# Turning the causal attention result to token-major by VectorE squares and a store and load through memory, in place of TensorE transposes

## The chip, the cores and the metric

The kernel runs on one core of one Trainium2 chip, in fp32. The metric is the device time of one execution in microseconds; the number to compare is the median of several executions. A core has TensorE (PE, with its weight loads listed as PEld), VectorE (DVE), ScalarE (ACT), GpSimd (POOL) and SyncE (SP), which here issues nearly all DMAs. Each engine works through its own queue in order.

## The reference, cut to what matters

A batch is 128 channels by 48 x 48 positions, that is 2304 tokens of 128 channels. There are 8 batches. For each of them:

```python
# layer 0
x1 = x + causal_attention(group_norm(x))      # q, k, v: leaky_relu of projections with position rows
# layer 1, over tokens t = x1 as [2304, 128]
t1 = t + softmax(n @ n.T) @ n                 # n = layer_norm(t)
t2 = t1 + ffn(layer_norm(t1))                 # projection, batch norm over all tokens, sigmoid recurrence over tokens
```

In the causal attention, `out[n] = sum over m <= n of softmax(q_n . k_m / sqrt(128)) v_m`. What matters for the change is its last step: the result comes out with channels on the partitions, but it is added to `x`, and normalized over the channels, with tokens on the partitions.

## The kernel before, in words

A batch is cut into 6 chunks of 384 tokens (`NQ`, `QC`), a chunk into 3 blocks of 128 (`QB`). A batch has a causal part (class `Causal`, layer 0) and a full part (class `Full`, the attention of layer 1). Both work on items: a pair of one query chunk `j` and one key block `m`. An item is a score product `s` (line 980), an exponential on ScalarE into a tile `p` (982), for blocks on the diagonal a mask on POOL (985), and a product with the values into the PSUM tile `o` (991). The scores lie transposed, keys on the partitions, so `o` has channels on the partitions and tokens along the free dimension. The sum of the exponentials, which softmax divides by, is gathered on VectorE: every `p` is added to `acc` (1002, 1006). Chunk `j` of the causal part has 3(j+1) items. The tiles `p` come from a pool of 6, the PSUM tiles of scores and projections from one of 4 (`psum_s`), small results and transposes from one of 2 (`psum_t`), `o` from one of 2. A fp32 matmul is two passes of TensorE in the trace.

When a causal chunk is complete, `after` copies `o` to SBUF on ScalarE (1015, in the order that makes later 32 x 32 blocks fit), starts the load of the token-major `x` of that chunk (`x_tok`, 1019), and adds a chain of six steps:

- `turn`: VectorE turns `acc` in squares of 32 and sums the rows (1023, 1025);
- `sums`: a small TensorE matmul `dn` sums over the squares, VectorE takes the reciprocal `ri` (1031 to 1036);
- `residual`: TensorE transposes the three blocks of the copy into PSUM (`oc_t`, 931), VectorE multiplies by `ri` and adds `x` (1042), and takes mean and variance (912, 913);
- `rooted`: POOL takes the root (921);
- `normed`: VectorE normalizes into `xhT` (926);
- `back`: TensorE transposes to channel-major (`tb`, 931), ScalarE copies it (1061).

The full part needs the normalized chunks of the same batch. It has a chain of its own for each finished chunk, with the same transposes (`of_t`), and spreads and fetches tiles by DMA through memory (1248 to 1257).

The order of the queues is written out by hand: the program emits instructions in the order in which a small planner, `Stream`, runs the steps. `stream` lists the items of all batches, and the product of an item comes three items after its scores (`LAG`). The planner keeps a clock `now`, advanced by the columns of each matmul (`US` each), and for VectorE, ScalarE and POOL a time from which they are free (`free`). A chain's step has a cost in TensorE time and a list of engine times; it may run when its time `at` has come, at most two steps per item, the oldest chain first. So changed steps or costs shift the order of the other instructions too. `chunk_tile` hands out a tile from a tag's ring and first runs the chain of the tile's earlier holder up to a given step, so that a tile is not taken before its readers are in the queues.

The causal part of a batch starts while the full part of the batch before is still ending: the projections of the new batch (`project`, 871 to 886), its first chunks, and the last chain of the old batch meet there.

VectorE's `transpose` turns each 32 x 32 square by itself. A 128 x 128 block so turned still has its 16 squares in the old places.

Of the kernel before, what the change touches and what calls it, by code (L numbers as in the profile page):

```python
# [14 lines left out]
F32 = mybir.dt.float32  # L15
AF = mybir.ActivationFunctionType
ALU = mybir.AluOpType
# [587 lines left out]
def fast_path(ctx: ExitStack, tc: tile.TileContext, x, pe, w_ffn, out, x_tok, w_qkv, w_pos, v_t, gamma_beta, flag):  # L605
    nc = tc.nc
    B, C, H, W = x.shape
    N = H * W
    P = 128
# [52 lines left out]
    with ExitStack() as actx:  # L662
# [107 lines left out]
        for r in roots:  # L770
            nc.gpsimd.memset(r, 0.0)

        st = Stream()
        order = ExitStack()
        order.enter_context(tc.manual_schedule())
# [5 lines left out]
        def group_norm(b):  # L781
            xt = xbuf[b]
            c = {}

            def part1():
                gs = small2.tile([P, NQ, 6], F32, tag="gn_st", name=f"gn_st_{b}")
                for j in range(NQ):
                    nc.vector.bn_stats(gs[:, j, :], xt[:, ts(j, QC)])
                mv = small.tile([P, 2], F32, tag="gn_mv", name=f"gn_mv_{b}")
                nc.vector.bn_aggr(mv, gs)  # L790
                c["mv"] = mv

            def part2():
                mv = c["mv"]
                tp = psum_t(f"gn_m_{b}")
                nc.tensor.matmul(tp[:, 0:1], grp, mv[:, 0:1], start=True, stop=True)
                mg = small.tile([P, 1], F32, tag="gn_mg", name=f"gn_mg_{b}")
# [3 lines left out]
                e = small.tile([P, 1], F32, tag="gn_e", name=f"gn_e_{b}")  # L801
                nc.vector.scalar_tensor_tensor(e, d, d, mv[:, 1:2], ALU.mult, ALU.add)
                c["mg"], c["e"] = mg, e

            def part3():
                tp = psum_t(f"gn_v_{b}")
                nc.tensor.matmul(tp[:, 0:1], grp, c["e"], start=True, stop=True)
                rs = small.tile([P, 1], F32, tag="gn_rs", name=f"gn_rs_{b}")
                rsqrt(small, rs, tp[:, 0:1], 1e-5, "gn")
# [90 lines left out]

        def bounds(b):

            qk = small.tile([P, 2], F32, tag="qk", name=f"qk_{b}")
# [47 lines left out]
        class Causal:  # L951
# [37 lines left out]
            def product(self, j, m, o, p, ready, first, last):  # L989
                b, off = self.b, self.offset(j, m)  # L990
                nc.tensor.matmul(o[:, off:QC], vals[b][:, ts(m, P)], p[:, off:], start=first, stop=last)  # L991
                st.spend((QC - off) * US, ready)

                if first:
                    self.sums[j] = (p, None)
                    return
                if self.sums[j][1] is None:
                    self.whose[j] = {}
                    a = chunk_tile("acc", f"acc_{b}_{j}", self.whose[j], 1)
                    if off:  # L1000
                        nc.vector.tensor_copy(a[:, :off], self.sums[j][0][:, :off])
                    nc.vector.tensor_add(a[:, off:], self.sums[j][0][:, off:], p[:, off:])
                    self.sums[j] = (None, a)
                else:
                    a = self.sums[j][1]
                    nc.vector.tensor_add(a[:, off:], a[:, off:], p[:, off:])  # L1006
                st.then(ready, [("DVE", 0.15 + (QC - off) * 0.00105)])

            def after(self, j, o):
# [1 line left out]
                cols = ts(j, QC)  # L1011
                acc = self.sums.pop(j)[1]
                c = self.whose.pop(j)
                o_sb = chunk_tile("o", f"oc_{b}_{j}", c, 3)
                nc.scalar.copy(by_block(o_sb), o[:, :QC].rearrange("p (a g r) -> p a g r", a=R, g=QB))
                at = st.then(st.now, [("ACT", 0.5)])

                y = t1p.tile([P, QC], F32, tag="t1t", name=f"t1t_{b}_{j}")
                nc.sync.dma_start(y, x_tok[b, j])
# [17 lines left out]
                    c["ri"] = ri  # L1037

                def residual():
                    to = transposed(o_sb, f"oc_t_{b}_{j}")  # L1040
                    for g in range(QB):
                        nc.vector.scalar_tensor_tensor(
                            y[:, ts(g, P)], to[:, ts(g, P)], c["ri"][:, g : g + 1], y[:, ts(g, P)], ALU.mult, ALU.add
                        )
                    t1_tok[b, j] = y
                    c["mv"], c["ve"] = moments(y, f"c{b}_{j}", "l1")
# [25 lines left out]
        class Full:  # L1072
# [115 lines left out]
            def after(self, j, o):  # L1188
                b, rows, tsum = self.b, self.rows, self.tsum
                cols = ts(j, QC)  # L1190
                c = {}
                o_sb = chunk_tile("o", f"of_{b}_{j}", c, 2)
                nc.scalar.copy(o_sb, o[:, :QC])
                at = st.then(st.now, [("ACT", 0.5)])
                last = b == B - 1 and j >= NQ - 2

                def sums():

                    dn = small.tile([P, QB], F32, tag="dn", name=f"dn_{b}_{j}")
                    nc.vector.tensor_reduce(dn, rows[:, QB * j : QB * (j + 1), : j + 1], AX.X, ALU.add)  # L1200
                    n = NQ - 1 - j
                    if n:
                        tp = psum_t(f"ts_{b}_{j}")
                        k = n * R * QB
                        nc.tensor.matmul(
                            tp[:, :k], same.rearrange("p a c -> p (a c)"), tsum[j][:, :n, :].rearrange("p n k -> p (n k)"),
                            start=True, stop=True,
                        )
                        own = small2.tile([P, NQ - 1, R, QB], F32, tag="own", name=f"own_{b}_{j}")
                        nc.vector.tensor_mul(  # L1210
                            own[:, :n].rearrange("p n a g -> p (n a g)"), tp[:, :k], mine[:, :n].rearrange("p n a g -> p (n a g)")
                        )
                        more = small.tile([P, QB], F32, tag="more", name=f"more_{b}_{j}")
                        nc.vector.tensor_reduce(more, own[:, :n].rearrange("p n a g -> p g (n a)"), AX.X, ALU.add)
                        nc.vector.tensor_add(dn, dn, more)
                    ri = small.tile([P, QB], F32, tag="ri", name=f"ri_{b}_{j}")
                    nc.vector.reciprocal(ri, dn)
                    c["ri"] = ri

                def residual():  # L1220
                    tp = transposed(o_sb, f"of_t_{b}_{j}")
                    t2 = chunk_tile("t2", f"t2_{b}_{j}", c, 5 if last else 2, bufs=1)
                    for g in range(QB):
                        nc.vector.scalar_tensor_tensor(  # L1224
                            t2[:, ts(g, P)], tp[:, ts(g, P)], c["ri"][:, g : g + 1], t1_tok[b, j][:, ts(g, P)], ALU.mult, ALU.add
                        )
                    c["t2"] = t2
                    c["mv"], c["ve"] = moments(t2, f"f{b}_{j}", "l2")
                    if not last:
                        c["tt"] = chunk_tile("turn", f"tt_{b}_{j}", c, 5, bufs=1)  # L1230
# [20 lines left out]
                        nc.sync.dma_start(d[r], c["tt"][ts(r, SQ)].rearrange("c (k f) -> c k f", k=R))  # L1251

                def fetch():
                    c["t2x"] = chunk_tile("t2x", f"t2x_{b}_{j}", c, 7, bufs=1)
                    nc.sync.dma_start(c["t2x"], t2_d[:, b, cols])
                    c["scale"] = chunk_tile("scale", f"scale_{b}_{j}", c, 8, bufs=1)
                    nc.sync.dma_start(c["scale"], c["rs_d"][0].partition_broadcast(P))

                def product():
# [56 lines left out]
                else:  # L1316
# [5 lines left out]
                        (stored, 0.0, [("ACT", 0.85)]),  # L1322
                    ]
                c["chain"] = self.before["chain"] = st.add([
                    (sums, 0.15, [("DVE", 0.8)]),
                    (residual, 0.35, [("DVE", 3.2)]),
                    (rooted, 0.0, [("POOL", 0.9)]),
                    *steps,
                ], max(at, st.free["DVE"]) + 0.2 - st.now)
# [236 lines left out]
```

## Time and profile before

| | |
|---|---|
| median of 3 executions | 1795.67 us (1794.95 to 1795.85) |
| profiled execution, its own time | 1795.9 us |
| its span | 1793.8 us |
| mean granted TensorE clock | 0.991 |
| PE busy | 1757.0 us, 98% |
| DVE busy | 1298.0 us, 72% |
| ACT busy | 751.6 us, 42% |
| POOL busy | 217.0 us, 12% |
| DMA moved | 240.35 MB, 134 GB/s over the span |

The span runs from the first to the last instruction of the profiled execution; its own time is 2.1 us more. A row of a group of instructions names the line, the engine, the operation, the tiles `out<-in`, the shape and the count, then the busy time, the mean duration of one in ns, and the idle time of the engine ahead of them with what ended it. A matmul's duration is longer than the distance to the next one, since matmuls are pipelined; distances are read from the starts in a timeline. A row of a wait says who waited for whom, the sum in us, the number of times and the longest.

### The profile page before, as it was taken

Reading aid. Unit: us, or ns where it says so; the run is one execution under the profiler, and the core shown is the slowest. Engines: PE = TensorE matmul, PEld = TensorE weight load, DVE = VectorE, ACT = ScalarE, POOL = GpSimd, SP = SyncE. Lnnn points to the kernel's source line nnn. Section 1 sums busy time; section 2 is a strip of 40 time slices with the busy share of each in tenths; the row PEclk is TensorE's granted clock in tenths of the full one; section 3 lists DMA queues with packets and bytes.
Section 4 is the critical chain, followed back from the end, with each engine's and each line's share of the span. In section 5 each row is a group of like instructions: output and inputs, shape, how many; then the busy total and the mean of one; then the engine's idle time right before and its main releaser. Section 6 shows DMA issues by size and latency. Waiting matters only on the chain.

```text
span 1793.8 us, 22009 instructions
## 1 busy us (share of the span) xinstructions
PE 1757.0 (98%) x6363; PEld 1106.4 (62%) x6363; DVE 1298.0 (72%) x3321; ACT 751.6 (42%) x1852; POOL 217.0 (12%) x305
## 2 busy tenths in 40 slices
PE   8999999999999999999999999999999999999995
PEld 5666566665666566665666656665666656665574
DVE  5768668766887668686687668876686866876477
ACT  2344434443345424444344433454234443444354
POOL 1100011000210002000110002100020001100016
PEclk8999999999999999999999999999999999999998
DMA  4205662257314583056622573145830566025857
GB/s 151 102 1 190 180 166 82 74 181 192 109 62 132 162 217 106 1 188 179 167 83 74 182 187 113 63 132 163 216 106 1 183 183 172 27 72 182 201 179 200
DMA packets 176774, 240.35 MB, mean 134 GB/s; under 512 B 66209, under 2 KB 146242, under 8 KB 176644
## 3 DMA queue, kind: packets, MB, share of 16 engines
q1 hardware_dynamic: 175692, 235.83, 44.7%
q0 software_dynamic: 720, 2.62, 1.0%
q8 instruction: 53, 0.87, 0.2%
q14 instruction: 77, 0.63, 0.1%
q10 hardware_dynamic: 232, 0.40, 0.1%
HBM read 142.37 MB, written 96.41 MB: 133 GB/s over the span
## 4 chain that ended last, share of the span: by engine, by line
PE 95%; DVE 2%; DMA 1%; SPq 1%; issue 1%; ACT 0%; POOL 0%; DVEq 0%; ACTq 0%; POOLq 0%
PE s L1168 18%; PE o L1182 18%; PE s L980 17%; PE o L991 16%; PE o L1178 12%; PE pj L871 4%; PE pj L874 2%; PE z L1483 2%; PE wx L1264 2%; PE oc_t L931 1%; PE tb L931 1%; PE of_t L931 1%; SPq L1102 1%; DVE r L1465 0%; PE pb L829 0%
## 5 line engine op out<-in xcount | busy, mean ns | idle before, releaser
L1170 ACT ACTIVATE p<-s,shift 128x384 f32<-128x384 f32 x504 | 293.1, 582 | 491.3 <-PE s L1168 482.4
L982 ACT ACTIVATE p<-s 128x384 f32<-128x384 f32 (+2 forms) x504 | 233.0, 463 | 426.2 <-PE s L980 389.1
L1168 PE MATMUL s<-xh 128*128 128x384 f32 x1008 | 410.3, 489 | 0.0
L1182 PE MATMUL o<-p,xhT 128*128 128x384 f32 x1008 | 403.9, 487 | 4.4 <-ACT p L1170 4.4
L980 PE MATMUL s<-q,k 128*128 128x384 f32 (+2 forms) x1008 | 381.4, 460 | 0.1
L991 PE MATMUL o<-p,vT 128*128 128x384 f32 (+2 forms) x1008 | 378.3, 457 | 0.0
L1178 PE MATMUL o<-g,xhT 128*128 128x384 f32 x720 | 281.5, 488 | 1.4 <-DMA g<-e 1.3
L1182 PEld LDWEIGHTS o<-p,xhT 128*128 128x128 f32 x1008 | 189.0, 190 | 132.3 <-ACT p L1170 8.7
L991 PEld LDWEIGHTS o<-p,vT 128*128 128x128 f32 x1008 | 189.0, 191 | 114.7 <-issue 0.6
L1168 PEld LDWEIGHTS s<-xh 128*128 128x128 f32 x1008 | 186.1, 190 | 115.0
L1006 DVE TENSOR_TENSOR acc<-acc,p 128x384 f32<-128x384 f32 (+2 forms) x408 | 211.1, 517 | 48.9 <-ACT p L982 18.0
L980 PEld LDWEIGHTS s<-q,k 128*128 128x128 f32 x1008 | 180.9, 191 | 90.8 <-issue 0.9
L1131 DVE STREAM_TRANSPOSE t<-p 128x384 f32<-128x384 f32 x360 | 187.3, 550 | 37.6 <-ACT p L1170 36.2
L1178 PEld LDWEIGHTS o<-g,xhT 128*128 128x128 f32 x720 | 133.0, 190 | 84.1 <-issue 2.7
L1139 DVE TENSOR_REDUCE tsum<-t 128x12 f32<-128x1152 f32 x120 | 162.3, 1353 | 4.2
L876 DVE TENSOR_TENSOR z<-pj,pb 128x384 f32<-128x384 f32 x144 | 79.0, 548 | 105.2 <-PE pj L871 88.3
L985 POOL TENSOR_TENSOR p<-p,triu 128x128 f32<-128x128 f32 x144 | 83.4, 586 | 547.6 <-ACT p L982 417.2
L1237 POOL TENSOR_TENSOR roots<-ve_f,mhalf 128x3 f32<-128x3 f32 x48 | 40.8, 849 | 553.0 <-DVE ve_f L915 553.0
L1170 ACT ACTIVATION_READ_ACCUMULATOR p<-s,shift 128x1 f32 x504 | 98.0, 194 | 0.0
L871 PE MATMUL pj<-xn,wT 128*128 128x384 f32 x192 | 80.4, 504 | 1.4 <-DVE xn L864 1.4
L921 POOL TENSOR_TENSOR rs_c<-ve_c,mhalf 128x3 f32<-128x3 f32 x48 | 46.9, 977 | 245.7 <-DVE ve_c L915 245.7
L1224 DVE SCALAR_TENSOR_TENSOR t<-of_t,ri,t1t 128x128 f32<-128x128 f32 x144 | 41.5, 343 | 33.2 <-PE of_t L931 33.2
(262 smaller groups left out, 1492.2 us busy)
## 6 DMA issues: line engine op xcount, KB each, us to landing
e<-t SPq DMA_DIRECT2D x120, 576.0 KB
g<-e SPq DMA_DIRECT2D x480, 144.0 KB
pb<-posb_d SPq DMA_DIRECT2D x46, 576.0 KB
t1t<-in_x_tok_dram SPq DMA_DIRECT2D x48, 192.0 KB
t_d<-tt SPq DMA_DIRECT2D x184, 48.0 KB
t2x<-t_d SPq DMA_DIRECT2D x46, 192.0 KB
scale<-rs SPq DMA_DIRECT2D x46, 192.0 KB
x<-in_x_dram SPq DMA_DIRECT2D x14, 576.0 KB
```

The source lines that it names most:

```text
L871: nc.tensor.matmul(ps[:, :QC], wT[:, j, :], xn, start=True, stop=True)
L980: nc.tensor.matmul(s[:, off:QC], keys[b][:, ts(m, P)], queries[b, j][:, off:], start=True, stop=True)
L982: nc.scalar.activation(p[:, off:], s[:, off:QC], AF.Exp, scale=SCALE)
L985: nc.gpsimd.tensor_mul(p[:, off : off + P], p[:, off : off + P], triu)
L991: nc.tensor.matmul(o[:, off:QC], vals[b][:, ts(m, P)], p[:, off:], start=first, stop=last)
L1006: nc.vector.tensor_add(a[:, off:], a[:, off:], p[:, off:])
L1131: nc.vector.transpose(t[:, :, :, g, :].rearrange("p b j r -> p j b r"), p.rearrange("p (j b r) -> p j b r", j=QB, b=R))
L1139: nc.vector.tensor_reduce(self.tsum[j][:, n - j - 1, :], t.rearrange("p b j m r -> p (b j) (m r)"), AX.X, ALU.add)
L1168: nc.tensor.matmul(s[:, :QC], xh[:, ts(m, P)], xh[:, ts(j, QC)], start=True, stop=True)
L1170: nc.scalar.activation(p, s[:, :QC], AF.Exp, bias=shift, accum_out=self.rows[:, m, j : j + 1])
L1178: nc.tensor.matmul(out_ap, xhT[:, QB * i + g, :], p, start=first, stop=last)
L1182: nc.tensor.matmul(o[:, :QC], xhT[:, what[1], :], p, start=first, stop=last)
```

## The change

For the causal chunks 0 to 4 of every batch (`CAUSAL_FAR`; chunk 5 stays as it was), ScalarE's copy of `o` and TensorE's three transposes go. VectorE turns `o` in squares straight from PSUM into a tile `ot` (`turn_result`), one DMA stores it to a DRAM tile, and four DMAs load it back so that the squares stand in their turned places (`token_major`): the loaded tile `to` has tokens on the partitions. Store and load are two new steps of the chain, each with a planned time of 5 us. The multiply-add of the residual then reads `to` in SBUF, in runs of 32 elements, instead of PSUM; its step has no TensorE cost. The same way is written for the full part, but is switched off there (`FULL_FAR` is False), so in the full part `far` is False and its step counts do not change. Some small tiles move from the pool with 3 buffers to the one with 2 (left out below).

```diff
+        CAUSAL_FAR, FULL_FAR = True, False
...
+        def turn_result(o, name, holder, blocks_first):
+
+            ot = chunk_tile("o", f"ot_{name}", holder, 1)
+            dst, src = ot.rearrange("p (a g c) -> p a g c", a=R, g=QB), o[:, :QC]
+            if blocks_first:
+                dst, src = dst.rearrange("p a g c -> p g a c"), src.rearrange("p (g a r) -> p g a r", a=R, g=QB)
+            else:
+                src = src.rearrange("p (a g r) -> p a g r", a=R, g=QB)
+            nc.vector.transpose(dst, src)
+            return ot
+
+        def token_major(holder, ot, name, tag, steps):
+
+            d = dpool.tile([P, QC], F32, tag=f"o_{tag}", name=f"o_d_{name}")
+
+            def store():
+                nc.sync.dma_start(d, ot)
+
+            def load():
+                holder["o"] = to = chunk_tile(tag, f"to_{name}", holder, steps, bufs=1)
+                src = d.rearrange("(k r) (a f) -> a r k f", r=SQ, a=R)
+                for r in range(R):
+                    nc.sync.dma_start(to[ts(r, SQ)].rearrange("r (k f) -> r k f", k=R), src[r])
+
+            return [(store, 0.0, [("", 5.0)]), (load, 0.0, [("", 5.0)])]
+
+        def block_of(to, g):
+
+            return to.rearrange("p (k g c) -> p g k c", g=QB, c=SQ)[:, g]
...
-                    a = chunk_tile("acc", f"acc_{b}_{j}", self.whose[j], 1)
+                    a = chunk_tile("acc", f"acc_{b}_{j}", self.whose[j], 2 if CAUSAL_FAR and j < NQ - 1 else 1)
...
-                o_sb = chunk_tile("o", f"oc_{b}_{j}", c, 3)
-                nc.scalar.copy(by_block(o_sb), o[:, :QC].rearrange("p (a g r) -> p a g r", a=R, g=QB))
-                at = st.then(st.now, [("ACT", 0.5)])
+
+                far = CAUSAL_FAR and j < NQ - 1
+                if far:
+                    ot = turn_result(o, f"c_{b}_{j}", c, False)
+                    at = st.then(st.now, [("DVE", 0.57)])
+                    through = token_major(c, ot, f"c_{b}_{j}", "toc", 5)
+                else:
+                    o_sb = chunk_tile("o", f"oc_{b}_{j}", c, 3)
+                    nc.scalar.copy(by_block(o_sb), o[:, :QC].rearrange("p (a g r) -> p a g r", a=R, g=QB))
+                    at = st.then(st.now, [("ACT", 0.5)])
+                    through = []
...
                 def residual():
-                    to = transposed(o_sb, f"oc_t_{b}_{j}")
+                    to = None if far else transposed(o_sb, f"oc_t_{b}_{j}")
                     for g in range(QB):
+                        yg = y[:, ts(g, P)]
+                        if far:
+                            yg = yg.rearrange("p (k c) -> p k c", k=R)
                         nc.vector.scalar_tensor_tensor(
-                            y[:, ts(g, P)], to[:, ts(g, P)], c["ri"][:, g : g + 1], y[:, ts(g, P)], ALU.mult, ALU.add
+                            yg, block_of(c["o"], g) if far else to[:, ts(g, P)], c["ri"][:, g : g + 1], yg, ALU.mult, ALU.add
                         )
...
                 c["chain"] = normed_chunks[b, j] = st.add([
+                    *through[:1],
                     (turn, 0.0, [("DVE", 1.05)]),
+                    *through[1:],
                     (sums, 0.15, [("DVE", 0.55)]),
-                    (residual, 0.35, [("DVE", 2.6)]),
+                    (residual, 0.0 if far else 0.35, [("DVE", 2.6)]),
```

More of the change, by code (lines that the diff above doesn't have):

```diff
@@ L788, in part1 @@
                     nc.vector.bn_stats(gs[:, j, :], xt[:, ts(j, QC)])
-                mv = small.tile([P, 2], F32, tag="gn_mv", name=f"gn_mv_{b}")
+                mv = small2.tile([P, 2], F32, tag="gn_mv", name=f"gn_mv_{b}")
                 nc.vector.bn_aggr(mv, gs)
@@ L796, in part2 @@
                 nc.tensor.matmul(tp[:, 0:1], grp, mv[:, 0:1], start=True, stop=True)
-                mg = small.tile([P, 1], F32, tag="gn_mg", name=f"gn_mg_{b}")
+                mg = small2.tile([P, 1], F32, tag="gn_mg", name=f"gn_mg_{b}")
                 nc.vector.tensor_copy(mg, tp[:, 0:1])
@@ L800, in part2 @@
                 nc.vector.tensor_sub(d, mv[:, 0:1], mg)
-                e = small.tile([P, 1], F32, tag="gn_e", name=f"gn_e_{b}")
+                e = small2.tile([P, 1], F32, tag="gn_e", name=f"gn_e_{b}")
                 nc.vector.scalar_tensor_tensor(e, d, d, mv[:, 1:2], ALU.mult, ALU.add)
@@ L807, in part3 @@
                 nc.tensor.matmul(tp[:, 0:1], grp, c["e"], start=True, stop=True)
-                rs = small.tile([P, 1], F32, tag="gn_rs", name=f"gn_rs_{b}")
-                rsqrt(small, rs, tp[:, 0:1], 1e-5, "gn")
+                rs = small2.tile([P, 1], F32, tag="gn_rs", name=f"gn_rs_{b}")
+                rsqrt(small2, rs, tp[:, 0:1], 1e-5, "gn")
                 norm_of[b] = c["mg"], rs
@@ L901, in bounds @@
         def bounds(b):
-            qk = small.tile([P, 2], F32, tag="qk", name=f"qk_{b}")
+            qk = small2.tile([P, 2], F32, tag="qk", name=f"qk_{b}")
             nc.vector.tensor_reduce(qk, largest[b], AX.X, ALU.max)
@@ L1191, in after @@
                 c = {}
-                o_sb = chunk_tile("o", f"of_{b}_{j}", c, 2)
-                nc.scalar.copy(o_sb, o[:, :QC])
-                at = st.then(st.now, [("ACT", 0.5)])
                 last = b == B - 1 and j >= NQ - 2
+                far = FULL_FAR and not last
+                if far:
+                    ot = turn_result(o, f"f_{b}_{j}", c, True)
+                    at = st.then(st.now, [("DVE", 0.57)])
+                    through = token_major(c, ot, f"f_{b}_{j}", "tof", 4)
+                else:
+                    o_sb = chunk_tile("o", f"of_{b}_{j}", c, 2)
+                    nc.scalar.copy(o_sb, o[:, :QC])
+                    at = st.then(st.now, [("ACT", 0.5)])
+                    through = []
+                F = len(through)
                 def sums():
-                    dn = small.tile([P, QB], F32, tag="dn", name=f"dn_{b}_{j}")
+                    dn = small2.tile([P, QB], F32, tag="dn", name=f"dn_{b}_{j}")
                     nc.vector.tensor_reduce(dn, rows[:, QB * j : QB * (j + 1), : j + 1], AX.X, ALU.add)
@@ L1212, in sums @@
                         )
-                        more = small.tile([P, QB], F32, tag="more", name=f"more_{b}_{j}")
+                        more = small2.tile([P, QB], F32, tag="more", name=f"more_{b}_{j}")
                         nc.vector.tensor_reduce(more, own[:, :n].rearrange("p n a g -> p g (n a)"), AX.X, ALU.add)
@@ L1220, in residual @@
                 def residual():
-                    tp = transposed(o_sb, f"of_t_{b}_{j}")
-                    t2 = chunk_tile("t2", f"t2_{b}_{j}", c, 5 if last else 2, bufs=1)
+                    tp = None if far else transposed(o_sb, f"of_t_{b}_{j}")
+                    t2 = chunk_tile("t2", f"t2_{b}_{j}", c, 5 if last else 2 + F, bufs=1)
                     for g in range(QB):
+                        aps = t2[:, ts(g, P)], t1_tok[b, j][:, ts(g, P)]
+                        if far:
+                            aps = [i.rearrange("p (k c) -> p k c", k=R) for i in aps]
                         nc.vector.scalar_tensor_tensor(
-                            t2[:, ts(g, P)], tp[:, ts(g, P)], c["ri"][:, g : g + 1], t1_tok[b, j][:, ts(g, P)], ALU.mult, ALU.add
+                            aps[0], block_of(c["o"], g) if far else tp[:, ts(g, P)], c["ri"][:, g : g + 1], aps[1], ALU.mult, ALU.add
                         )
@@ L1229, in residual @@
                     if not last:
-                        c["tt"] = chunk_tile("turn", f"tt_{b}_{j}", c, 5, bufs=1)
+                        c["tt"] = chunk_tile("turn", f"tt_{b}_{j}", c, 5 + F, bufs=1)
                         nc.vector.transpose(
@@ L1253, in fetch @@
                 def fetch():
-                    c["t2x"] = chunk_tile("t2x", f"t2x_{b}_{j}", c, 7, bufs=1)
+                    c["t2x"] = chunk_tile("t2x", f"t2x_{b}_{j}", c, 7 + F, bufs=1)
                     nc.sync.dma_start(c["t2x"], t2_d[:, b, cols])
-                    c["scale"] = chunk_tile("scale", f"scale_{b}_{j}", c, 8, bufs=1)
+                    c["scale"] = chunk_tile("scale", f"scale_{b}_{j}", c, 8 + F, bufs=1)
                     nc.sync.dma_start(c["scale"], c["rs_d"][0].partition_broadcast(P))
@@ L1324, in after @@
                 c["chain"] = self.before["chain"] = st.add([
+                    *through,
                     (sums, 0.15, [("DVE", 0.8)]),
-                    (residual, 0.35, [("DVE", 3.2)]),
+                    (residual, 0.0 if far else 0.35, [("DVE", 3.2)]),
                     (rooted, 0.0, [("POOL", 0.9)]),
```

## The prediction

> **What bounds the kernel now.** I read the engines' busy shares first, then TensorE's own waits, then the timeline of one causal part (batch 2, 450 to 545 us), then the queue of SyncE.
>
> ```profile
> PE 1757.0 (98%) x6363; PEld 1106.4 (62%) x6363; DVE 1298.0 (72%) x3321; ACT 751.6 (42%) x1852; POOL 217.0 (12%) x305
> ...
> PE pw L1508 <- DVE off L1503: 11.7, 1, 11.7
> PE o L1182 <- ACT p L1170: 4.4, 7, 0.6
> ...
> 475.00:480.00 5.00, 5.00 (x22) 3.31 (x22) 4.89 (x16) 1.10 (x3) 1.71 (x2) 1.00 0.40 124
> 490.00:495.00 5.00, 5.00 (x25) 3.58 (x24) 4.76 (x13) 1.89 (x4) 0.65 (x1) 1.00 0.53 134
> 540.00:545.00 5.00, 5.00 (x17) 2.90 (x16) 1.86 (x4) 2.59 (x8) 0.00 (x0) 1.00 0.00 2
> ```
>
> TensorE is the bound. It is busy 98% of the span. Its longest wait is the 11.7 us at the very end, and its largest wait inside the eight batches is 4.4 us in all. In the windows (columns: PE, PEld, DVE, ACT, POOL busy, then granted clock, DMA share, GB/s) PE is busy 5.00 of 5.00 at clock 1.00. So what leaves TensorE's queue in a causal part comes off the time, unless another engine then makes it wait. VectorE is the only candidate: 4.89 and 4.76 of 5 us at the start of a causal part, though 1.86 at its end.
>
> **Removed: the TensorE transposes, on the path.** The changed program's queues show 40 groups of three transposes gone (5 chunks in each of 8 batches; chunk 5 keeps its own).
>
> ```profile
> L931 PE MATMUL oc_t<-ident,oc 128*128 128x128 f32 x144 | 23.6, 273 | 0.0
> ...
> 492.31 0.83 PE L874 MATMUL pj<-wT,xn 128*128 128x128 f32 x6
> 492.98 0.49 PE L931 MATMUL oc_t<-ident,oc 128*128 128x128 f32 x3
> 493.31 0.81 PE L980 MATMUL s<-q,k 128*128 128x384 f32 x2
> ```
>
> A transpose lasts 273 ns, but matmuls are pipelined: the group of three starts at 492.98 and the next matmul at 493.31. TensorE gives 0.33 us to a group, 0.109 to one. Here a rule speaks against the change: the Trainium skill, "VectorE: DVE Perf Modes", Rules for kernel authors, says to transpose 128x128 on TensorE where PSUM is acceptable as destination, since VectorE turns only 32x32 blocks; and "TensorE: Matmul & The Clock Gate", Part 4, prices a transpose in a kernel at about 275 ns. With that price the change would save 120 x 0.275 = 33 us (an estimate from that page), with the pitch 120 x 0.109 = 13.1 us. The row's duration agrees with the page, but in a queue without gaps only the pitch counts. I take 13.1 us.
>
> **Removed: 40 ACT copies (L1015, 479 ns).** They are 19 us of an engine that is 42% busy and mostly waits for TensorE. I count nothing; if ScalarE were late, this would be a gain, so it has no cost side.
>
> **Added on VectorE: 40 squares transposes out of PSUM.** No row shows this from PSUM. Near rows are the same instruction from SBUF, and a pair of additions that differ in where they read:
>
> ```profile
> L1131 DVE STREAM_TRANSPOSE t<-p 128x384 f32<-128x384 f32 x360 | 187.3, 550 | 37.6 <-ACT p L1170 36.2 <-DMA e<-t 0.8 <-issue 0.2
> L1006 DVE TENSOR_TENSOR acc<-acc,p 128x384 f32<-128x384 f32 x320 | 180.6, 564 | 36.5 <-ACT p L982 18.0 <-DVE acc L1006 0.5
> L876 DVE TENSOR_TENSOR z<-pj,pb 128x384 f32<-128x384 f32 x144 | 79.0, 548 | 105.2 <-PE pj L871 88.3 <-PE pj L874 9.3 <-DMA pb<-posb_d 5.1
> L1042 DVE SCALAR_TENSOR_TENSOR t1t<-oc_t,ric,t1t 128x128 f32<-128x128 f32 x144 | 41.4, 342 | 28.7 <-PE oc_t L931 28.7
> ```
>
> A PSUM source costs no more (548 against 564), so about 0.55 us each and 0.50 from start to start; bounds 0.5 and 0.7. In all 20 us, 2.5 us in a batch. The three multiply-adds of the residual now read SBUF in runs of 32; by the same pair I take them as unchanged, at 342 ns (bounds: 40 ns less or more, 5 us of VectorE time in all either way). VectorE's 28.7 us of waiting for `oc_t` go, five sixths of them with this change. All of that is beside TensorE, except where VectorE has no room.
>
> **Where VectorE has no room.** One place per batch, for batches 1 to 7, where the projections, the last residual of the batch before and the first causal chunks meet:
>
> ```profile
> 485.39 0.49 ACT L982 ACTIVATE p<-s 128x384 f32<-128x384 f32 x1 [1.96 <-DVE acc L1006]
> ...
> 486.69 0.81 PE L991 MATMUL o<-p,vT 128*128 128x384 f32 x2
> ```
>
> The exponential of chunk 3's second item waits 1.96 us for a `p` buffer that an addition on VectorE must free; it ends at 485.88, and its product starts at 486.69. Only 0.81 us is left before TensorE would stop. The change adds two squares here, but it also moves the order: in the new queue the residual of chunk 0 stands behind six additions of chunk 2 instead of before them, so this buffer comes free earlier and the tight spot moves on. I add the new queues from the projection of chunk 4. TensorE gets to it at 468.22 (dn and one score product no longer stand before it), and VectorE can start 0.93 us later, at 469.15 (0.645 for the two passes, 0.28 to reach VectorE, both as in the trace of before). All prices are start to start, from rows of this stretch. VectorE to the end of chunk 5's second projection add: 5 z at 0.59, 4 multiply-max at 0.48, 2 maxima at 0.46, 11 additions 4.7, 2 row-sum turns at 1.08, 2 squares at 0.5, the residual of the batch before 2.8, that of chunk 0 2.2, scale and statistics 1.4 with a short wait, small ones 1.1: 21.1 us from 469.15, done at 490.25. That add frees the PSUM bank that the scores of chunk 3's sixth direct item need, and TensorE comes to those after 28 matmuls of 0.645, 5 of 0.43, 4 of 0.22 and 1.14 of others, at 490.45. So 0.2 us is left, 0.5 us for the `p` buffers just ahead of it, and 0.65 us at the PSUM tile of the previous batch's transposes. VectorE instructions that coincide with POOL's masks ran up to 0.3 us long in the trace (one multiply-max 0.86 against 0.56), so I expect TensorE to wait about 0.25 us: 7 x 0.25 = 1.75 us. Bounds: nothing, and 1 us each (7 us).
>
> **Added on the queues: 40 stores of 192 KB and 160 loads of 48 KB, all on SyncE.** A near row is the turned store of L1251 (four of 48 KB, 384-byte runs) and the load that waits for it:
>
> ```profile
> 665.62 1.86 SPq L1251 DMA_DIRECT2D t_d<-tt  x4
> 669.30 0.34 SPq L1255 DMA_DIRECT2D t2x<-t_d  x1
> ```
>
> Four issues take 1.86 us, and the last has landed 1.8 us later: 3.7 us for the new loads, 0.43 + 1.8 = 2.2 us for the new store, 6 us the way round. Its cover is the place of the residual in VectorE's queue. In the new order the load of chunk 0 is issued some 18 us before its residual. The tightest is chunk 3: one buffer holds the loaded result, so its loads wait for chunk 2's residual to be read (about 517.7), land about 521.4, and VectorE comes to the residual about 523.4, after the square of chunk 4. That is 2 us of cover. If it were gone, VectorE would stand before additions that free `p`, and TensorE behind them has another 2.5 to 3.8 us (the exponential's end to its product, in this trace). The new store makes SyncE wait for VectorE's square; behind it stand the next batch's x, token tiles and position tiles, needed 20 us and more later. The four loads also stand ahead of the previous batch's last spread and fetch; the product that takes the fetched tile is some 10 us behind. DMA engines are nearly idle here (0.00 to 0.5 of the windows). I count nothing. The `small` to `small2` edits take a buffer from values that are written once per batch: nothing.
>
> **Sum.** Profiled execution 1795.9 us (span 1793.8 and 2.1 around it), 0.2 above the median. 1795.9 - 13.1 + 1.75 = 1784.5; against the median 1784.3. I say 1784.5.
>
> **Rivals.** (a) VectorE is later than I added up: the tight spot costs 1 us or more per batch. For it: 4.89 of 5 us busy, 0.2 us of spare. Against: order moved in its favour, and a wait of TensorE lets VectorE catch up. 1795.9 - 13.1 + 7 = 1789.8. (b) The way through memory is late, and the kernel is slower: the load of the next x (two of 576 KB, their packets ran from 493.5 to about 498.5) or SyncE's own wait holds the result back 5 us beyond its cover at two chunks of a batch. TensorE's slack takes 3, so 2 x 2 x 7 = 28 us: 1810.8. It decides from 13.1 / 7 = 1.9 us of TensorE waiting per batch. Against: x is issued well ahead of the loads of chunk 2. (c) The time does not change, since the saved slots turn into waits of TensorE for ScalarE or VectorE later in the batch: 1795.7. For it: seven waits for ScalarE exist already (4.4 us). Against: the order in the full part is the same in both programs.
>
> **How the numbers follow.** Main case 0.78, (a) 0.12, (b) 0.05, (c) 0.05. A measurement tells about 0.2% (3.6 us) from no change. The main case and (a) are both beyond it: faster 0.90, same 0.05, slower 0.05. The range goes from the whole 13.1 and 1 us more (startup may shift) to the end of (a): 1781.5 to 1790.
>
> **What would show it.** Right: 24 `oc_t` matmuls instead of 144, TensorE busy about 1744, a span of about 1782.5, and no new row above 3 us in TensorE's waits. Rival (a): new TensorE waits on VectorE or ScalarE, seven times, near the products of each batch's chunk 3. Rival (b): VectorE waiting at L1084 for the DMA `to<-o_d`, above 2.5 us at one time. The forecast is wrong if TensorE's idle time grows by over 5 us, or if the causal parts shorten by less than 1.2 us each.

## The result and the profile after

| | before | after |
|---|---|---|
| first measurement, median of 4 each | 1795.51 us (1794.95 to 1795.85) | 1780.54 us (1780.26 to 1782.23) |
| second measurement, medians of 19 and 6 | 1794.73 us (1792.81 to 1799.89) | 1781.95 us (1781.3 to 1784.22) |
| profiled execution, its own time | 1795.9 us | 1782.23 us |

The ratio is 0.9919 with an interval of 0.9902 to 0.9936 in the first measurement, and 0.9926 (0.9914 to 0.9938) in the second: the change makes the kernel 0.7 to 0.8% faster, 15.0 us by the first medians and 12.8 us by the second. The forecast of 1784.5 had the direction and the main term; the measured 1780.54 lies 1.0 us below the low end of its range (1781.5).

The page of the changed kernel, engines and TensorE's waits (the columns of a wait are sum in us, times, longest):

```profile
PE 1743.5 (98%) x6242; PEld 1093.8 (61%) x6243; DVE 1312.9 (74%) x3361; ACT 735.2 (41%) x1812; POOL 204.9 (12%) x305
...
PE pw L1564 <- DVE off L1559: 11.7, 1, 11.7
PE o L1226 <- ACT p L1214: 4.4, 7, 0.6
```

TensorE is 13.5 us less busy (1757.0 before), and its waits (the view lists idle times from 0.15 us on) are those of before: 11.7 us at the end, seven waits for ScalarE of 4.4 us in all, nothing new above 2 us. VectorE is 14.9 us busier. The span, 1780.2 us, is 13.6 shorter.

The groups that the change touches, in the same profile:

```profile
L932 PE MATMUL oc_t<-ident,oc 128*128 128x128 f32 x24 | 3.9, 273 | 0.0
L951 DVE STREAM_TRANSPOSE ot_c<-o 128x384 f32<-128x384 f32 x40 | 23.2, 579 | 11.8 <-PE o L1022 11.8
L1084 DVE SCALAR_TENSOR_TENSOR t1t<-to_c,ric,t1t 128x128 f32<-128x128 f32 x120 | 34.8, 344 | 0.7
L1084 DVE SCALAR_TENSOR_TENSOR t1t<-oc_t,ric,t1t 128x128 f32<-128x128 f32 x24 | 6.9, 345 | 5.4 <-PE oc_t L932 5.4
...
484.89 0.58 DVE L951 STREAM_TRANSPOSE ot_c<-o 128x384 f32<-128x384 f32 x1
485.39 0.52 DVE L1033 TENSOR_TENSOR acc<-p,p 128x384 f32<-128x384 f32 x1
```

The square out of PSUM takes 579 ns and, in the timeline (last two lines), 0.50 us from start to start. The multiply-add costs the same from SBUF in runs of 32 (344 ns) as from PSUM (345). None of the 0.7 us of idle time before it is put down to a load: the way through memory is covered everywhere.

The gain is regular. One place of TensorE's queue, the short wait for ScalarE (L1182 before, L1226 after), comes once in each of the first seven batches. Its first two, before and then after:

```profile
201.47 0.91 PE L1182 MATMUL o<-p,xhT 128*128 128x384 f32 x2 [0.63 <-ACT p L1170]
410.77 0.91 PE L1182 MATMUL o<-p,xhT 128*128 128x384 f32 x2 [0.62 <-ACT p L1170]
...
199.26 0.91 PE L1226 MATMUL o<-p,xhT 128*128 128x384 f32 x2 [0.63 <-ACT p L1214]
406.93 0.91 PE L1226 MATMUL o<-p,xhT 128*128 128x384 f32 x2 [0.63 <-ACT p L1214]
```

From one to the next, which is called the batch period below, takes 209.30 us before and 207.66 us after, in four and five of the six steps to within 0.02 us (the rest are up to 0.6 us longer). The difference is 1.64 us, that is 15 transposes at 0.109 us.

### The profile page after: what moved, and what is told of

The parts are those of the page before. It is cut to its first block, busy times and chain, and to the rows that moved or that the text cites. A ratio compares the mean times of both kernels' runs of the same rounds, so it can differ in the third digit from the quotient of the medians.

```text
span 1780.2 us, 22179 instructions
## 1 busy us (share of the span) xinstructions
PE 1743.5 (98%) x6242; PEld 1093.8 (61%) x6243; DVE 1312.9 (74%) x3361; ACT 735.2 (41%) x1812; POOL 204.9 (12%) x305
## 4 chain that ended last, share of the span: by engine, by line
PE 96%; DMA 1%; DVE 1%; issue 0%; ACT 0%; SPq 0%; POOL 0%; ACTq 0%; DVEq 0%; POOLq 0%
PE s L1212 18%; PE o L1226 18%; PE s L1011 17%; PE o L1022 17%; PE o L1222 12%; PE pj L872 4%; PE pj L875 2%; PE z L1539 2%; PE wx L1319 2%; PE tb L932 1%; PE of_t L932 1%; DVE r L1521 0%; PE pb L830 0%; DMA g<-e 0%; DMA x<-in_x_dram 0%
## 5 line engine op out<-in xcount | busy, mean ns | idle before, releaser
L1226 PE MATMUL o<-p,xhT 128*128 128x384 f32 x1008 | 403.9, 487 | 4.4 <-ACT p L1214 4.4
L1226 PEld LDWEIGHTS o<-p,xhT 128*128 128x128 f32 x1008 | 189.0, 190 | 132.3 <-ACT p L1214 8.7
L1016 POOL TENSOR_TENSOR p<-p,triu 128x128 f32<-128x128 f32 x144 | 72.8, 507 | 607.9 <-ACT p L1013 514.2
L1320 DVE TENSOR_TENSOR scale<-wx,scale 128x384 f32<-128x384 f32 x46 | 25.4, 552 | 56.3 <-PE wx L1319 56.3
```

What stands on the lines that cost most here:

```text
L1226: nc.tensor.matmul(o[:, :QC], xhT[:, what[1], :], p, start=first, stop=last)
```

## The experiments

### The same kernel again, one half alone, and the transposes put back

`after_again` is the changed kernel in more executions.

> The changed kernel once more, unchanged, in more executions. The profiled execution of it took 1782.23 us, its three others 1780.26 to 1780.8; the sum of the forecast without its 1.75 us of waits is 1782.8. Theory S (start-up): the gain in the eight batches is the 13.1 us of the transposes and no more; what executions differ by beyond that lies in the first 50 us, where the granted clock falls below 1.00, so spans of one program differ by up to 2 us, the longer ones at the lower mean clock, and the difference of the two kernels, over more executions, is 13 to 14.5 us. Theory G (a further gain): the change saves some 2 us more in the batches, in every execution; then the profiled execution taken now has a batch period shorter than 207.66 us, and the difference stays at 15 us. Rival C: the gain of 13 us is by chance of the chip; it is not there again.

Measured: 1781.95 us (1781.3 to 1784.22) against 1794.73, 12.8 us less; the batch period is 207.67 us. So there is no further gain in the batches: Theory S, with a difference just under its 13 to 14.5.

`pe_only` is the kernel before without the 120 transposes:

```diff
-                    to = transposed(o_sb, f"oc_t_{b}_{j}")
+                    to = o_sb if j < NQ - 1 else transposed(o_sb, f"oc_t_{b}_{j}")
```

> The kernel before, with the 120 oc_t transposes of chunks 0 to 4 left out and nothing else: ScalarE still copies o, the residual reads that copy as it stands (so these chunks are added channel-major, which is not the reference's result), and there is no square, no store and no load. The planner's costs stay, so the order of the queues is that of before. Theory S: this is the whole of the gain: 1795.5 - 13.1 = 1782.4, within 1 us of the changed kernel, and the TensorE waits for ScalarE of the kernel before are unchanged. Theory G: the order of the queues or the absent 40 copies give some 2 us beyond that, and this kernel is slower than the changed one by 1.5 to 2.5 us. Rival (c) of the prediction, saved slots turning into waits: 1790 or more.

Measured: 1782.34 us (1780.72 to 1783.66), ratio 0.9925 (0.9914 to 0.9937), batch period 207.66 us. Leaving out the transposes alone gives the whole gain. The 40 squares, the 200 DMAs, the 40 absent copies and the new order of the queues, which the changed kernel has besides, together change nothing that can be measured.

`pe_back` is the changed kernel with the transposes back, on a constant:

```diff
+                    if far:
+                        tp = psum_t(f"again_{b}_{j}")
+                        for g in range(QB):
+                            nc.tensor.transpose(tp[:, ts(g, P)], ident, ident)
```

> The changed kernel with three TensorE transposes put back at each of the 40 residuals (of a constant, into a PSUM tile that nothing reads), beside the way through memory, which stays. By the pitch of 0.109 us: 120 x 0.109 = 13.1 us more than the changed kernel, 1793.6, 0.735% up. By the duration of 0.275 us: 33 us more, 1813.5. If TensorE had waits left that the transposes can fill: under 10 us more.

Measured: 1794.78 us (1792.36 to 1798.6), which is the time of the kernel before: ratio 0.9997 (0.9989 to 1.0005). The batch period is 209.26 us, so 15 transposes cost 1.60 us, 0.107 us each. The duration of 0.273 us that each row shows would have given about 1815 (1781.95 + 120 x 0.273).

These runs also tell what the 15.0 us of the first measurement were made of: 13.1 us of transposes, and start-up. `after` and `after_again` are the same program, but the place that marks the batch period stands at 199.26 us in batch 0 of one and at 198.33 in the other. The columns of the rows are PE, PEld, DVE, ACT and POOL busy, granted clock, DMA share, GB/s; the first two are of the changed kernel's first profile, the last two of its second:

```profile
30.00:40.00 10.00, 10.00 (x30) 5.14 (x29) 4.76 (x11) 2.77 (x6) 0.00 (x0) 0.72 0.24 79
40.00:50.00 10.00, 8.56 (x35) 4.66 (x33) 7.55 (x16) 2.14 (x6) 1.36 (x3) 1.00 0.34 119
...
30.00:40.00 10.00, 10.00 (x36) 5.30 (x34) 5.10 (x12) 3.40 (x7) 0.00 (x0) 0.92 0.27 86
40.00:50.00 10.00, 8.57 (x34) 5.01 (x34) 7.57 (x16) 2.10 (x5) 1.36 (x3) 1.00 0.34 113
```

The granted clock of the first 50 us differs from execution to execution (0.72 against 0.92 in the same 10 us), and behind it the batches run at 1.00. For the executions without a profile only the mean clock is on record, and it goes the same way: 0.993 in the one of 1780.26 us, 0.990 in the one of 1784.22. So an execution moves by a few us with its start, and the two medians of the changed kernel, 1780.54 and 1781.95, are 1.4 us apart. That the first four came out near the short end is luck.

### How much room VectorE has

Each square is done twice, three or four times; the copies write the same values to the same place.

```diff
-            nc.vector.transpose(dst, src)
+            for _ in range(3):
+                nc.vector.transpose(dst, src)
```

> The changed kernel with each of the 40 squares out of PSUM done twice (the second overwrites the first with the same values): 20 us more of VectorE, 0.50 us from start to start each. Theory W (the walk through the queues holds, only its 0.3 us for the masks was wrong): in the trace of the changed kernel, batch 2, the projection add of key chunk 5 ends at 486.37 and the scores that need its PSUM bank start at 486.72, so 0.35 us is left. Two squares stand ahead of it in that stretch; the first extra one is met by a 0.34 us wait of VectorE for TensorE (wx), so VectorE is 0.50 - 0.34 + 0.50 = 0.66 us later there and TensorE waits 0.31 us in each of seven batches: 2.2 us, 1784 (4.6 us, 1786.5, if that wait absorbs nothing). New TensorE waits for VectorE at s. Theory N (the tight spot has more room than the walk says, for example the 1.7 us between exponential and product): no change, 1782, no such waits.

Measured: 1783.22 us (1781.79 to 1783.84), no new wait of TensorE in the list, batch period 207.65 to 207.96. Theory N: the wait that the prediction expected from VectorE does not come even with a second square. The timelines of VectorE and TensorE in this kernel, batch 2, show why:

```profile
488.92 0.55 DVE L877 TENSOR_TENSOR z<-pj,pb 128x384 f32<-128x384 f32 x1
...
488.28 0.59 PE L1023 MATMUL o<-p,vT 128*128 128x256 f32 x2
488.72 0.81 PE L1012 MATMUL s<-q,k 128*128 128x384 f32 x2
489.36 0.38 PE L1023 MATMUL o<-p,vT 128*128 128x128 f32 x2
489.64 0.91 PE L1012 MATMUL s<-q,k 128*128 128x384 f32 x2
```

The scores that the prediction's walk named (chunk 3 with block 5) start at 488.72, while the addition that was said to free their PSUM bank runs from 488.92 to 489.47. So these scores use another bank. In TensorE's queue of the changed kernel, the first scores behind that addition that carry a wait for VectorE are two items and 2.2 us later, those of block 7.

> The changed kernel with each of its 40 squares done three times. With two, TensorE did not wait, and the room between the exponential of chunk 3's first remaining item and its product fell from 1.74 to 1.00 us per batch (0.80 in batch 2). Theory P (the narrow place is the p buffer of that item, freed by an addition that stands behind the squares of chunks 1 and 2; 1.74 us of room): one more square each takes 2 x 0.50 us, so the room ends at 0.0 us, -0.2 in batch 2: no wait or next to none, 1782 to 1784. Theory N (there is still much more room): the room stays above 0.5 us.

Measured: 1789.88 us (1789.14 to 1791.78), 7.9 above `after_again`, with TensorE waiting at two places of batches 1 to 7. Theory P named one of them, but put the wait at nothing.

> The changed kernel with each of its 40 squares done four times. Theory P: room of 1.00 - 2 x 1.0 = -1.0 us, so TensorE waits 1.0 us for ScalarE or POOL at chunk 3 in each of seven batches: 7 us, 1789, somewhat more if the granted clock falls after the waits. Theory N: no wait, 1782 to 1784.

Measured: 1803.51 us (1802.27 to 1805.73), 21.6 above, three times the 7 us expected. The waits of `square_three`, then those of `square_four`, and for the first of the two places ScalarE's and TensorE's timelines in batch 2 of the changed kernel and TensorE's of `square_four`:

```profile
PE s L1012 <- ACT p L1014: 2.8, 7, 0.7
PE of_t L932 <- DVE ownc L1073: 1.4, 7, 0.2
...
PE s L1012 <- ACT p L1014: 6.8, 7, 1.0
PE of_t L932 <- DVE ownc L1073: 6.3, 7, 1.2
...
486.00 0.98 ACT L1013 ACTIVATE p<-s 128x384 f32<-128x384 f32 x2 [0.66 <-DVE acc L1033]
487.58 0.81 PE L1011 MATMUL s<-q,k 128*128 128x384 f32 x2
...
495.59 0.91 PE L1012 MATMUL s<-q,k 128*128 128x384 f32 x2 [0.97 <-ACT p L1014]
```

Once the room is gone, the price shows: the batch period is 208.70 us with three squares and 210.31 with four, 1.0 and 2.65 more than 207.66. The listed waits come to less (0.6 us a batch with three squares), since idle time counts from the end of the matmul before, and matmuls overlap. Three squares cost more than expected for three reasons.

- There are two narrow places and not one. The second is the PSUM tile of the previous batch's transposes `of_t`, which the `dn` product holds until VectorE has read it (`ownc`). The prediction had put 0.65 us of room there; in the changed kernel `ownc` ends at 473.90 and `of_t` starts at 474.76, so it is 0.86. My expectation for three squares had left this place out.
- At the first, the `p` buffer behind the squares of chunks 1 and 2, the expectations measured the room to the wrong instruction. They took the product with the values, at 488.23: 1.74 us behind the exponential, 1.00 with two squares. But TensorE's waits there are of scores (`s` for ScalarE), which stand just ahead of that product in its queue, at 487.58, and which start 0.05 us after that exponential has ended whenever they wait (an exponential reads a PSUM tile that later scores take). The exponential ends at 486.49 (the first of the two of 0.49 us in the row), so the room is 1.09 us. With two squares it is 0.30 to 0.36, and in batch 2 the exponential ends at 489.59 and the scores start at 489.64: nothing is left.
- A repeated square takes VectorE 0.61 us from the start of the one before, not 0.50.

### How much room the way through memory has

In `hop_twice` each loaded tile is stored and loaded once more, in `hop_thrice` twice more (the diff is of `hop_thrice`; in it the squares change places twice, so that they end where they were, other than its expectation says).

```diff
+                for _ in range(2):
+                    nc.sync.dma_start(d, to)
+                    for r in range(R):
+                        nc.sync.dma_start(to[ts(r, SQ)].rearrange("r (k f) -> r k f", k=R), src[r])
```

> The changed kernel, in which each loaded result is stored and loaded once more before it is used (40 stores of 192 KB and 160 loads of 48 KB more, on the same queue; chunks 0 to 4 so come out with squares in other places, which is not the reference's result). Each way is some 6 us longer. In the trace of the changed kernel the last load of a chunk is issued 20, 13, 13, 6 and 11.6 us ahead of the residual of chunks 0 to 4, and landing takes 2.2 of it: only chunk 3 has less than 6 us of cover, 3.8. Theory C (cover): VectorE waits about 2.1 us for the load at chunk 3 of each batch, and the 2.5 us between exponential and product takes it, so 1782 to 1784. Theory Q (any longer way shows, at the residual or in what stands behind on SyncE's queue): TensorE waits 2 us or more per batch, above 1797.

Measured: 1785.58 us (1784.94 to 1788.93), 3.6 above `after_again`. The batch period is still 207.66 us. VectorE's wait and TensorE's in this kernel:

```profile
DVE t1t L1087 <- DMA to_c<-o_d_c: 13.5, 8, 5.6
...
PE tb L932 <- DVE xhT L927: 2.6, 1, 2.6
```

In batches 1 to 7 VectorE waits about 1.1 us ((13.5 - 5.6) / 7) at chunk 3, and TensorE has no wait that the changed kernel lacks: Theory C, with half the wait that I had put. The loss is at one place of batch 0, where cover is shorter than in the other batches (7.1 and 7.9 us from the last load to the residual of chunks 2 and 1, against 13) and where chunk 2's last load, whose buffer waits for chunk 1's residual, goes out 12.0 us behind the start of that residual (2.2 in the changed kernel); I had only looked at the batches behind it.

> As hop_twice, but with two further ways through memory instead of one: some 12 us longer than in the changed kernel (the result of chunks 0 to 4 is again not the reference's). By the same covers: chunk 3 is 8.2 us late, chunk 4, whose loads wait for chunk 3's residual, some 8 us, chunks 1 and 2 about 1 us. Theory C: VectorE waits 16 us per batch, TensorE has 2.5 to 3.5 us of room at each, so it stops for some 5 us at two places of each batch: 80 us or more, 1860. If the extra loads wait out of the way of everything but the residual, and the additions are not behind it: below 1800.

Measured: 1893.24 us (1889.5 to 1900.58), 111 above. VectorE waits 152.1 us for the loads, and TensorE's waits behind it are 29.7 us for POOL, 20.9 for ScalarE, 17.0 for VectorE at `tb` and 5.2 at `dn`. So lateness does decide, in batches 1 to 7 from somewhere between 6 and 12 us beyond the present way.

### More of the same change

The switched-off way for the full part was turned on, for 46 of its 48 chunks, then for the first two, then for the sixth alone; and for the sixth causal chunk. The loaded tiles of both parts share one buffer where both are in use.

```diff
-        CAUSAL_FAR, FULL_FAR = True, False
+        CAUSAL_FAR, FULL_FAR = True, True
...
-                holder["o"] = to = chunk_tile(tag, f"to_{name}", holder, steps, bufs=1)
+                holder["o"] = to = chunk_tile("to", f"to_{name}", holder, steps, bufs=1)
```

> The changed kernel with the same way for the full part too (46 of its 48 chunks; the loaded tiles of both parts share one buffer, for lack of room for two). Removed: 138 of_t transposes, 138 x 0.109 = 15.0 us of TensorE, and 46 ScalarE copies. Added: 46 squares of 0.50 us on VectorE (23 us, from 1313 to 1336 of 1765 us) and 46 ways through memory. Theory S (only TensorE's pitch counts while VectorE and memory have cover): 1780.5 - 15.0 = 1765.5. Rival T (tight spot): one square more in the stretch where the next batch's projections meet the last residuals, where 0.35 us is left in the trace of after: TensorE waits 0.2 to 1 us in each of seven batches, 1767 to 1772.5. Rival M (memory late): the one buffer, or the 6 us way, holds the last full residual back and with it the additions behind it: above 1775.

Measured: 1816.09 us (1813.12 to 1817.18), slower than before (ratio 1.0112, 1.0098 to 1.0126). The main wait is not for VectorE:

```profile
PE o L1222 <- DMA g<-e: 26.1, 9, 4.0
...
236.18 0.88 PE L1222 MATMUL o<-g,xhT 128*128 128x384 f32 x2 [3.29 <-DMA g<-e]
```

The first line is of TensorE's waits, the second of its timeline in batch 1. `g<-e` is the load of a turned tile for the next product, in SyncE's queue. Around it (windows of this kernel, columns as above):

```profile
234.00:236.00 2.00, 0.00 (x0) 0.00 (x0) 0.00 (x0) 0.00 (x0) 0.00 (x0) 1.00 1.09 256
238.00:240.00 2.00, 2.00 (x5) 1.08 (x4) 1.12 (x2) 0.60 (x2) 0.00 (x0) 0.50 1.08 244
```

The DMA engines are full there (share 1.0), and after the wait TensorE gets a clock of 0.50. But full engines alone do not explain the wait: in the changed kernel their share from 215 to 230 us is 0.96 to 0.99, and TensorE does not stop. What differs is SyncE's queue, where a store and four loads of a result now stand between the spreads and fetches, and where the store `e<-t` of the next turned tiles is issued at 228.13 us instead of 219.25 (the batch itself starts 4 us later).

> The kernel with the way through memory in both parts, but in the full part for chunks 0 and 1 alone. With all chunks of the full part it took 1816.09 us: TensorE waited once per batch, 3 to 4 us, for the load g<-e of a turned tile (26.1 us in all), behind which its clock was granted at 0.50 for some microseconds; that wait is where SyncE's queue and the DMA engines (share 1.0) are full, at full chunks 3 and 4. Theory F (the wait comes from the DMA load of that stretch): chunks 0 and 1 end where the DMA share is 0.6, so their 16 groups of transposes come off and nothing is added: 1782 - 16 x 0.327 = 1776.8. Theory P (the full part can't take a way through memory at all, for example through VectorE's squares or the shared buffer): TensorE waits in each batch as before, above 1785.

Measured: 1810.23 us (1805.61 to 1812.7), so Theory F falls, at least in its form "only chunks 3 and 4 do harm". The wait is for the same load (`g<-e`, 27.5 us, 17 times), and again where full chunks 3 and 4 are worked on. In this kernel's SyncE queue two spreads of seven DMAs stand between 191 and 207 us, where the changed kernel has one, and the store `e<-t` ahead of the late load is issued at 227.65 instead of 219.25. The chains of chunks 0 and 1 have two steps more, so their later DMAs have moved into the crowded stretch. That this order is the cause, here and in `both_far`, I have argued from the queue; no run isolates it.

For `full5` the condition is `FULL_FAR and not last and j == NQ - 1`.

> The kernel with the way through memory for chunks 0 to 4 of the causal part and for the sixth chunk of the full part (7 of its 8; the loaded tiles of both parts share one buffer). That chunk's way falls into the next batch's causal part, where SyncE issues DMAs for 0 to 3 us in 10 (7 to 8 in 10 at full chunks 2 to 4). Theory Q (what hurt with the full part's chunks was SyncE's full queue ahead of g<-e, and nothing else): 21 transposes less, 21 x 0.109 = 2.3 us, 1779.7, and no TensorE wait for g<-e beyond the 1.5 us of the changed kernel. Theory B (the shared buffer or the longer chain moves VectorE's queue into the tight spot, or the spread falls on the next turned tiles): TensorE waits by 1 us or more per batch, 1787 or more.

Measured: 1793.49 us (1791.28 to 1797.98), 11.5 above `after_again`. The wait for `g<-e` is small (3.3 us), as Theory Q says, but Theory B's comes instead: TensorE waits 7.2 us in six places for POOL's `p`, up to 1.3 us, where the next batch's chunk 3 is. Behind POOL stands VectorE again: at the place in batch 2 the exponential ahead of the mask starts at 487.25 after 2.26 us of waiting for an addition. Whether the square, the two added steps or the shared buffer put that addition late is not shown.

In `six`, `far = CAUSAL_FAR` without the exception of the sixth chunk.

> The changed kernel with the way through memory for the sixth causal chunk too: 24 more transposes of TensorE go, 24 x 0.109 = 2.6 us. In the trace of the changed kernel (batch 1) the last product of that chunk is at 331.0, its residual starts at 337.5, its normalized chunk is copied at 346.9 to 347.4, and the full part's 16th score product, which needs it, starts at 348.0: 0.6 us of room, where the other chunks have a whole chunk of TensorE work ahead of theirs. Square, store and loads take 0.6 + 2.2 + 3.7 us after the product, so the residual starts near 338.5, 1 us later, and TensorE waits some 0.4 to 1 us in each of eight batches: 3 to 8 us against 2.6 gained, 1782 to 1787, with waits of s for ScalarE's xh. Rival (the way has cover here as well): 1779.4, no such waits.

Measured: 1839.54 us (1837.45 to 1842.63), 57.6 above `after_again`, far beyond the 3 to 8 us expected. TensorE's timeline in batch 1, and the granted clock there:

```profile
354.03 0.29 PE L1070 MATMUL dn<-parts,same 128*128 128x12 f32 x2
358.84 0.90 PE L932 MATMUL tb<-ident,xhT 128*128 128x128 f32 x3 [4.53 <-DVE xhT L927]
360.31 1.65 PE L1212 MATMUL s<-xh 128*128 128x384 f32 x2 [0.57 <-ACT xh L1103]
...
358.00:360.00 2.00, 0.90 (x3) 0.55 (x3) 1.65 (x5) 0.23 (x1) 0.32 (x1) 0.50 0.00 0
```

The last load is issued at 345.35 and VectorE has no listed wait for it, so memory was done some 6 us before `dn` at 354; the row sums that `dn` reads were done at 345.38. What is late is the order: `dn` stands late in TensorE's queue. From the planner's rule I take the reason: it gives store and load 5 us each, puts `dn` behind them, and the scores force the rest of the chain into the queues directly before themselves. No run with another planned time shows this. From `dn` over reciprocal, residual, root and normalization to `tb` there are then 4.5 us with nothing between. The half clock takes 2.5 us more (5.34 us from 358.84 to 364.18, against 0.33 of transposes, 0.57 of wait for ScalarE and three pairs at 0.645 = 2.84). With these, 4.53 + 0.57 + 2.5, a batch loses 7.6 us and gains 0.33: 8 x 7.3 = 58, as measured.

None of these variants beat the changed kernel. It takes the way through memory at the five chunks where it is covered.

## Why the prediction was right and wrong

1. **TensorE as bound, 13.1 us by the pitch: right.** The profile after shows 24 `oc_t` matmuls and 1743.5 us of TensorE (forecast about 1744). `pe_only` and `pe_back` give the gain and take it back, at 0.109 and 0.107 us a transpose. The rule of the Trainium skill ("VectorE: DVE Perf Modes", Rules for kernel authors) to transpose on TensorE did not hold for the end to end time here: with TensorE 98% busy, three of its transposes cost 0.327 us that show, and one square costs 0.50 us on VectorE that do not.
2. **ScalarE's copies and the multiply-adds at nothing: right** (`pe_only` keeps the copies and is as fast; 344 against 345 ns).
3. **The squares: right in size** (0.50 us from start to start, 579 ns each; bounds were 0.5 to 0.7).
4. **The wait of 0.25 us in seven batches, 1.75 us: wrong, and this is the step of the sum that failed.** There is no such wait. VectorE's part of the walk came out exactly (21.1 us forecast, 465.23 to 486.37 = 21.14 in the profile after). But the walk ended at the wrong scores. It took the bank to be needed by the sixth direct item, at 486.72, and these scores do not wait for VectorE, as `square_twice` shows. If the bank goes to the first scores that do, at 488.88, the room was 2.5 us, not 0.2; the trace does not name banks. What is narrow in the changed kernel is the PSUM tile of `of_t` (0.86 us; forecast 0.65) and the scores behind the `p` buffer (1.09 us; forecast 0.5 at the buffers); neither makes TensorE wait. The 0.3 us for coincidence with POOL's masks was not seen either: the multiply-max that took 0.86 us in each of batches 1 to 7 before takes at most 0.56 us in all of them after.
5. **The way through memory at nothing: right.** Cover at chunk 3 was larger than forecast (6.0 us from the last load's issue to the residual, some 4 beyond landing, since in `hop_twice`, where the residual waits for the load, it starts 2.0 us after the last issue; forecast 2). Rival (b) would have needed a way about 6 to 12 us longer.
6. **The rivals: none came.** (a) would have needed new waits at chunk 3; they are listed only from the third square on. (c) would have shown in `pe_only`.
7. **The range: too narrow below, by the term for the start.** Its low end had no wait in it, only the 13.1 us and 1 us for start-up, so the missing wait alone would not have put the result outside. Of the 4.0 us between 1784.5 and 1780.54, 1.75 are the wait; the other 2.3 (1782.8 without the wait, against 1780.54) are scatter between executions, by the clocks above mostly of the start; the sum took it from one execution of 1795.9 us, the longest of its four. The changed program ran from 1780.26 to 1784.22 us over ten executions, the mean granted clock going the same way, and the profiled one took 1782.23. The second median, 1781.95, lies inside the range. A range around one profiled execution has to hold that scatter on both sides.

## What to carry to other kernels

Price an instruction on the engine that bounds the kernel by its pitch in a gapless queue, and on the others by the room in the narrowest stretch; find that room by walking the queues, and check in the queue which instruction really waits for the buffer before you put a number on the wait. A longer way through memory was free here where it started early and the DMA queue was idle, and new steps in a chain move everything behind them: the same change that gained 0.7% at five chunks lost wherever else it was tried. When a profile has room, repeating the added instruction, twice and more, is a cheap way to measure it.

## What the runs showed of the hardware

A long wait of TensorE costs more than itself. After a wait of 4.53 us (`six`) it was granted a clock of 0.50 for about 5 us, and after one of 2.61 us (`hop_twice`, batch 0) for about 3 us; the window from 106 to 108 us of `hop_twice` shows it. After waits of 0.82 and 0.97 us (`square_four`) the clock stayed at 1.00. In between the length does not decide alone: after waits of 3.01 us (`both_far`, 1081.96) and 2.41 us (`far_first2`, 239.68) it stayed at 1.00, and after one of 1.99 us (`far_first2`, 1292.71) it was 0.50 for about 3 us.

```profile
106.00:108.00 2.00, 2.00 (x5) 1.09 (x5) 1.70 (x4) 0.90 (x2) 0.00 (x0) 0.50 0.34 82
...
494.00:498.00 4.00, 3.03 (x12) 1.78 (x11) 3.65 (x9) 1.99 (x5) 0.00 (x0) 1.00 0.02 4
```

The second row is of `square_four`, with its wait of 0.97 us inside. This is part of why `six`, `both_far` and `hop_thrice` lost more than the sums of their waits: in `hop_thrice` TensorE is 1781.9 us busy with the work that takes it 1743 in the changed kernel.
